# A norm ahead of the block numbers, and routing's second product behind the next transposes

## The chip, the core and the metric

The kernel runs on one core of a Trainium2 chip. The time is the device time of one execution in microseconds. The engines named below are TensorE (PE: matrix products and transposes; PEld is its load of the stationary operand), VectorE (DVE), ScalarE (ACT), GpSimd (POOL) and SyncE (SP, which only issues transfers and reads registers). TensorE writes its results to PSUM, of which the kernel uses 8 banks.

## What is computed

The input x holds 2 sequences of 2048 tokens with 256 channels, in float32. A feed-forward layer, an attention and the same feed-forward layer again are added to it. Cut to what matters:

```python
x = x + 0.5 * ffn(layernorm(x))
x = x + attention(layernorm(x))        # causal, one head of 128
x = x + 0.5 * ffn(layernorm(x))

def ffn(y):
    xln = ln(y, ln1)
    x1 = y + (sigmoid(xln @ Wr) * (xln @ Wv)) @ Wo
    h = ln(x1, ln2)
    conf = sigmoid(h @ [conf_rwkv, conf_trans])          # 3 experts
    bids = conf * shares * sigmoid(h @ w_diff) + h @ W_aff
    w = argmax(bids)                                      # one expert a token
    scale = conf[w] / (conf[w] + 1e-6)
    out = square(relu(h @ K[w])) @ V[w]                   # w = 0, 1
    out = (h @ W1 * sigmoid(xln @ Ws @ W2)) @ W3          # w = 2
    return x1 + out * scale
```

## The kernel before

**Stages.** The feed-forward layer is split. `front` (line 756) does all up to the choice of the expert, in groups of 512 tokens (4 tiles of 128 rows); the two sequences are segments of 4 groups each, so `front` runs over 8 groups, numbered 0 to 7 here. It writes each token's row into a place of its expert in a DRAM table (`move`, an indirect transfer on POOL). `experts` (line 844) then reads blocks of 256 rows that want the same expert, runs the expert and writes the results back by token number. `finish` (line 599) stands at the end of a segment: from the number of tokens of each expert it works out, in some 20 small operations on DVE, `steer`, the numbers of the blocks. SP reads these to address the blocks' rows (`load_rows`, tile `rows_in`). For the first segment that is `finish_whole` (line 626).

**One group in `front`.** While group i is chosen for, group i + 1 is projected and group i + 2 is begun. The steps that this text names:
- `route(0)` (line 464): 8 small products of y_t, the transposed normed rows, with the routing weights, into the sums `ps_rc`. They stay open.
- `rank` for group i - 1: two products, of its winners and of the running counts `upto`.
- `mix`: gate_t times Wo, in two halves `acc`, each a sum over two passes (k = 0, 1). DVE adds them to the rows (line 455).
- `route(1)`: the second product, of gate_t, onto the same `ps_rc`; ACT copies the sum to `by_col` and the token ids to the rows (lines 482, 483).
- `columns` (line 417): 8 transposes of the rows of group i + 1 into two tiles `ps_t`, each copied to `y_t` by ACT.
- `deviation`: moments of the new rows on DVE; `r(0)`: 4 products with Wr and a sigmoid; `start`: moments of group i + 2; `slot`, `move` for group i - 1; `norm2`, `logits`: a transpose of `by_col` (`ps_route`) and small DVE work; `v(0)`: 4 products with Wv, then gate_t on DVE (line 436); `choose`: some 12 small DVE operations ending in `upto`; `r(1)`, `v(1)`.
- At the last group of a segment: `rank`, `slot`, `move` and `finish`.
- `norm1` for group i + 2: six small DVE operations (lines 305 to 318), then its rows are normed on ACT, one tile after another (line 322). Where its group has no row buffer with the input in it, it also has SP copy the input there (line 408, in the second layer).

**Banks.** There are two PSUM pools: `p_mm` with 6 banks (tag "mm") for products and `p_tp` with 2 (tag "tp") for transposes and small sums. A tile waits until one of its pool's banks is free.

**Order.** In the first layer, up to `AHEAD` = 10 steps of `front` beyond the end of the first segment, PE, DVE and ACT keep the order in which the program names the work. From there on a planner orders each engine's work: it plays the program with modelled costs and takes what is ready, what the program names first going first. `front` is a generator; each `yield` ends a step. Beside `experts`, three steps of `front` (`PACE`) go with one of `experts`. In the second layer, `front` for segment 0 is interleaved with the attention of the other sequence. There a row of scores is 128 queries against up to 2048 keys, in up to four tiles `ps_s`; `ps_o` sums the values, and `ps_pt` are the transposes of the probabilities.

Of the kernel before, what the change touches and what calls it, by code (L numbers as in the profile page):

```python
# [8 lines left out]
F32 = mybir.dt.float32  # L9
# [7 lines left out]
P = 128  # L17
# [39 lines left out]
def run(steps):  # L57
    for _ in steps:
        pass
# [20 lines left out]
def kernel(ctx: ExitStack, tc: tile.TileContext, a: dict, out: bass.AP):  # L80
# [6 lines left out]
    GB = T // TG  # L87
# [14 lines left out]
    p_mm = ctx.enter_context(tc.tile_pool(name="p_mm", bufs=6, space=PSUM))  # L102
    p_tp = ctx.enter_context(tc.tile_pool(name="p_tp", bufs=2, space=PSUM))
# [273 lines left out]
    class Group:  # L377
# [86 lines left out]
        def route(self, part):  # L464


            if part == 0:
                self.ps_c = p_tp.tile([P, P], F32, name="ps_rc", tag="tp")
            w, src = ((route_y, self.y_t), (route_g, self.gate_t))[part]
            for k in range(KC):  # L470
                for t in range(TB):
                    nc.tensor.matmul(
                        self.ps_c[t * RC : (t + 1) * RC, :],
                        lhsT=w[:, k, :],
                        rhs=src[:, k, t * P : (t + 1) * P],
                        start=part == 0 and k == 0,
                        stop=part == 1 and k == KC - 1,
                    )
            if part == 0:
                return  # L480
            self.by_col = self.work.tile([P, P], F32, name="by_col")
            nc.scalar.copy(self.by_col, self.ps_c)
            nc.scalar.copy(
                self.rows[:, :, ID], self.seg["ids"][:, self.n * TB : (self.n + 1) * TB]
            )
# [113 lines left out]
    def finish(seg):  # L599

        ps = p_tp.tile([P, E], F32, name="ps_n", tag="tp")
        nc.tensor.matmul(ps, lhsT=ones, rhs=seg["upto"][:, :, ST], start=True, stop=True)
        n_of = sort_pool.tile([P, E], F32, name="n_of")
        nc.vector.tensor_sub(n_of, ps, first[:, :, 0])
        steer = sort_pool.tile([P, STEER], I32, name="steer", bufs=6)

        seg["skip"] = sort_pool.tile([P, STEER], F32, name="skip", bufs=3) if seg["prior"] is not None else None
        if seg["prior"] is None:
            finish_whole(seg, n_of, steer)
        else:  # L610
            for _ in finish_rest(seg, n_of, steer):

                yield from [None] * PACE
        seg["steer"], seg["n_of"] = steer, n_of
        yield
# [140 lines left out]
    def front(work, segs, by_exp=-1, on_move=lambda: None, fill=()):  # L756


        todo = [
            Group(work, seg, n, (b * GB + n <= by_exp, b * GB + n < by_exp)) for b, seg in enumerate(segs) for n in range(GB)  # L760
        ]

        def at(i):
            return todo[i] if 0 <= i < len(todo) else None

        def move(group):
            group.move()
            on_move()

        todo[0].start()  # L770
        run(todo[0].norm1(TB // 2, lately.get("p_tr") if by_exp >= 0 else None))
        yield
        todo[1].start()
        todo[0].columns()
        yield
        for m in range(KC):
            todo[0].r(m)
            yield
            todo[0].v(m)
            yield  # L780
        run(todo[1].norm1(0))
        for i, this in enumerate(todo):
            late, following, further = at(i - 1), at(i + 1), at(i + 2)
            if late and late.n == GB - 1:
                late = None
            this.route(0)
            if late:
                late.rank()
                yield
            this.mix()  # L790
            yield
            this.route(1)
            if following:
                following.columns()
                yield
            this.deviation()
            yield
            if following:
                following.r(0)
                yield  # L800

            if further:
                further.start()
                yield
            if late:
                late.slot()
                with tc.issue_after((further or this).guess):
                    move(late)
                yield
            this.norm2(late.made if late else None)  # L810
            this.logits()
            yield
            if following:
                following.v(0)
                yield
            if following or "gated" not in lately:
                this.choose()
            else:

                for _ in range(PAUSE):  # L820
                    yield
                this.choose(lately["gated"])
            yield
            if following:
                following.r(1)
                yield
                following.v(1)
                yield
            if this.n == GB - 1:

                yield from fill
                if not following:
                    for _ in range(PACE):
                        yield
                this.rank()
                this.slot()
                yield
                move(this)
                yield from finish(this.seg)
            if further:  # L840
                yield from further.norm1(0, following.made)
                yield

    def experts(work, segs, dest, leftovers=False):

# [419 lines left out]
    def until_placed(steps, seg):  # L1265
        while "steer" not in seg:
            next(steps)
            yield
# [5 lines left out]
    def second_half(n, front_pool, segs):  # L1274

        t0, t1 = segs
        with pool(f"attention{n}", "right") as work:
            for g in range(GB):
                x = front_pool.tile([P, TB, C], F32, name=f"x{g}")
                wait_for(nc.sync.dma_start(x, token_tiles(x_mid, GB + g)).ins, s0["results"] + s1["results"])  # L1280
                t1["x"].append(x)
            units = [work.tile([P, TG], F32, name=f"prob{u}") for u in range(5 * GB)]
            xns = [work.tile([P, TB, C], F32, name=f"xn{i}") for i in range(2)]
            xts = [work.tile([P, KC, TG], F32, name=f"x_t{i}") for i in range(2)]
            normed_rows = [r[:, :, YN : YN + C] for r in t0["rows"]]

            def halves(tiles):
                return [t[:, i : i + 2, :] for t in tiles for i in range(0, TB, 2)]


            other = attention(work, t1["x"], units, halves(xns), xns, xts)
            for i, _ in enumerate(attention(work, t0["x"], units, halves(normed_rows[0:2]), xns, xts, normed_rows)):
                if i in NEXT_AT:
                    next(other)
            following = front(front_pool, [t0, t1], by_exp=GB)
            interleave(other, until_placed(following, t0), 9, 8)
            advance(following, AHEAD)
# [10 lines left out]
    with ExitStack() as second:  # L1308
        with pool("experts0", "right") as expert_pool:
            with pool("front0", "left") as front_pool:  # L1310
# [29 lines left out]
                def next_x():  # L1340
                    if waiting:
                        n = waiting.pop(0)
                        fetch(front_pool, s1, n, x_of(1, n), GB + 2)
                        if not waiting:
                            nothing_yet(1)
                            for e in range(E):
                                nc.sync.dma_start(
                                    slot_rows(by_slot[1], e * REGION, NI), blank.unsqueeze(1).to_broadcast([P, NI, RW])
                                )

                following = front(front_pool, [s0, s1], on_move=next_x, fill=folding)
                with tc.manual_schedule(engines={nc.tensor.engine, nc.vector.engine, nc.scalar.engine}):

# [14 lines left out]
                following = until_placed(following, s1)  # L1368
# [76 lines left out]
```

## Time and profile before

The median of 3 runs is 871.15 us (869.32 to 871.39). The profiled execution took 870.89 us by the clock of the runs; its span, from the first to the last instruction, is 869.2 us.

| stage (us from the span's start) | TensorE busy | DVE busy | ACT busy | granted clock |
|---|---|---|---|---|
| first layer, front alone, 28 to 60 (32.0) | 31.62 | 24.55 | 12.53 | 1.00 |
| end of segment 0, 60 to 100 (40.0) | 38.26 | 33.28 | 13.53 | 0.96 |
| front beside experts, 100 to 160 (60.0) | 59.10 | 42.61 | 24.31 | 1.00 |
| experts, 160 to 300 (140.0) | 139.17 | 54.63 | 50.57 | 1.00 |
| attention, 330 to 500 (170.0) | 164.37 | 105.07 | 72.03 | 1.00 |
| attention beside front, 500 to 620 (120.0) | 117.92 | 81.75 | 45.93 | 1.00 |
| front beside experts, 620 to 690 (70.0) | 68.61 | 49.28 | 28.26 | 1.00 |
| experts, 690 to 860 (170.0) | 168.15 | 56.22 | 55.38 | 1.00 |

How to read the lines shown later. A line of the timeline is: start in us, length in us, engine, line of the kernel, operation, what it writes <- what it reads, its size, xcount (how many in a row), and in brackets how long the engine was idle before and what ended that. A matrix product of float32 appears as two instructions, so "x4" for an output of 512 columns are two products. The ends of products are modelled and overlap the next start, so lengths on TensorE are best read from start to start. A line of the page's slices has one digit for a fortieth of the span, the busy share in tenths.

### The profile page before, as it was taken

How to read it: one execution, taken by the hardware profiler on the slowest of the kernel's cores; microseconds unless marked ns; L12 is line 12 of the kernel's file. 1: busy time of each engine (PE TensorE's matmuls, PEld its weight loads, DVE VectorE, ACT ScalarE, POOL GpSimd, SP SyncE). 2: the span in 40 equal slices, each digit the busy share in tenths (PEclk: the TensorE clock that was granted, in tenths of full speed). 3: DMA queues.
4: the chain of work that ended last, by engine and by line, in shares of the span. 5: the costliest groups of instructions: out<-in, count | busy, mean ns of one | idle time of the engine just before them, and what ended most of it. 6: DMA issues, size and time to landing. Idle time of an engine off the chain costs nothing. (4 is left out here: it accounts for less than half of the span.)

```text
span 869.2 us, 12422 instructions
## 1 busy us (share of the span) xinstructions
PE 836.5 (96%) x4136; PEld 612.8 (71%) x4136; DVE 468.8 (54%) x1858; ACT 319.8 (37%) x694; POOL 185.3 (21%) x232
## 2 busy tenths in 40 slices
PE   5999999999999999999999999999999999999995
PEld 4556567888888887555566556556566888888884
DVE  3588866423334645687364777664875523333321
ACT  3243451323443333354363353522362233342311
POOL 3135244311022122000010103033233501112110
PEclk9999999999999999999999999999999999999998
DMA  9924724937269453000000001021373955538641
GB/s 306 373 99 170 266 112 158 365 125 257 91 223 356 170 182 100 0 1 0 1 1 1 1 0 74 25 97 74 130 260 110 370 188 173 191 121 276 216 172 55
DMA packets 69241, 128.09 MB, mean 147 GB/s; under 512 B 4782, under 2 KB 46638, under 8 KB 69168
## 3 DMA queue, kind: packets, MB, share of 16 engines
q1 hardware_dynamic: 58736, 91.93, 31.2%
q0 software_dynamic: 8384, 33.70, 9.7%
q10 hardware_dynamic: 2048, 1.58, 0.6%
q8 instruction: 34, 0.56, 0.3%
q14 instruction: 39, 0.32, 0.1%
HBM read 82.47 MB, written 43.15 MB: 145 GB/s over the span
## 5 line engine op out<-in xcount | busy, mean ns | idle before, releaser
L895 PE MATMUL acc<-w_e,hid 128*128 128x256 f32 x704 | 156.9, 379 | 0.0
L880 PE MATMUL ps_b<-cols,w_k 128*128 128x256 f32 (+1 forms) x768 | 156.5, 362 | 0.0
L880 PEld LDWEIGHTS ps_b<-cols,w_k 128*128 128x128 f32 x768 | 136.4, 190 | 16.6
L895 PEld LDWEIGHTS acc<-w_e,hid 128*128 128x128 f32 x704 | 131.3, 190 | 17.3 <-DVE hid L1023 0.6
L293 POOL TENSOR_TENSOR r<-ve,mhalf 128x4 f32<-128x4 f32 (+1 forms) x40 | 51.3, 1283 | 353.9 <-DVE ve L334 238.2
L1022 ACT ACTIVATE relu<-ps_b 128x512 f32<-128x512 f32 x88 | 52.0, 591 | 165.5 <-PE ps_b L880 163.2
L1023 DVE TENSOR_TENSOR hid<-ps_b,relu 128x512 f32<-128x512 f32 x88 | 60.7, 690 | 77.6 <-ACT relu L1022 76.3
L920 DVE SCALAR_TENSOR_TENSOR res<-acc,rows_in 128x256 f32<-128x256 f32 x68 | 30.2, 479 | 117.4 <-PE acc L895 117.4
L1210 PE MATMUL ps_o<-p_tr,v 128*128 128x512 f32 (+3 forms) x160 | 72.8, 539 | 4.1 <-ACT p_tr L1202 2.3
L572 POOL DMA_INDIRECT by_slot<-rows,slots x64 | 63.0, 985 | 30.3 <-issue 24.8
L928 POOL DMA_INDIRECT out_dram<-res,where x34 | 33.4, 981 | 157.6 <-DVE res L920 133.6
L365 PE MATMUL ps_p<-y_t,w_r 128*128 128x512 f32 x128 | 64.4, 625 | 1.0 <-ACT y_t L420 1.0
L1156 PE MATMUL ps_s<-k_t,q_t 128*128 128x512 f32 (+3 forms) x160 | 64.0, 529 | 0.0
L365 PE MATMUL ps_p<-y_t,w_v 128*128 128x512 f32 x128 | 62.6, 607 | 0.1
L928 POOL DMA_INDIRECT x_mid<-res,where x34 | 33.5, 986 | 133.0 <-DVE res L920 117.0
L446 PE MATMUL acc<-w_o,gate_t 128*128 128x256 f32 x256 | 59.5, 384 | 0.0
L1165 DVE TENSOR_REDUCE top<-ps_s 128x1 f32<-128x512 f32 (+2 forms) x80 | 48.5, 607 | 15.4 <-PE ps_s L1156 14.4
L1173 ACT ACTIVATE prob<-ps_s,shift 128x512 f32<-128x512 f32 (+3 forms) x64 | 38.2, 605 | 43.7 <-DVE shift L1169 43.6
L446 PEld LDWEIGHTS acc<-w_o,gate_t 128*128 128x128 f32 x256 | 47.3, 190 | 7.0 <-issue 0.8
L357 ACT ACTIVATE cols<-ps_bt,lnp 128x256 f32<-128x256 f32 (+1 forms) x96 | 47.3, 553 | 13.2 <-PE ps_bt L864 12.7
L1156 PEld LDWEIGHTS ps_s<-k_t,q_t 128*128 128x128 f32 x160 | 29.2, 190 | 29.3 <-issue 26.3
L283 DVE BATCH_NORM_STATS2 stats<-rows 128x6 f32<-128x256 f32 x128 | 46.3, 412 | 5.0 <-DMA rows<-in_x_dram 5.0
(236 smaller groups left out, 1136.3 us busy)
## 6 DMA issues: line engine op xcount, KB each, us to landing
w_k<-in_K_rwkv_dram SPq DMA_DIRECT2D x24, 1024.0 KB, 6.9
w_e<-in_V_rwkv_dram SPq DMA_DIRECT2D x24, 1024.0 KB, 8.1
rows_in<-by_slot SPq DMA_DIRECT2D x20, 516.0 KB, 6.5
rows_in<-by_slot SPq DMA_DIRECT2D x12, 772.0 KB, 5.5
by_slot<-rows_in SPq DMA_DIRECT2D x6, 772.0 KB, 10.7
rows<-in_x_dram SPq DMA_DIRECT2D x8, 512.0 KB, 5.3
x_mid<-rows_in SPq DMA_DIRECT2D x2, 2048.0 KB, 17.4
rows<-x_mid SPq DMA_DIRECT2D x4, 512.0 KB, 9.5
```

The costliest lines, as they stand in the source:

```text
L293: guess = nc.gpsimd.tensor_tensor(r0[:, 0:n, :], ve[:, 0:n, :], mhalf[:, 0:n, :], ALU.pow)
L365: nc.tensor.matmul(ps, lhsT=w[:, k, m * P : (m + 1) * P], rhs=src_t[:, k, :], start=k == 0, stop=k == KC - 1)
L446: nc.tensor.matmul(acc[:, i, :], lhsT=self.gate_t[:, k, t * P : (t + 1) * P], rhs=w_o[:, k, :], start=k == 0, stop=k == KC - 1,)
L572: nc.gpsimd.indirect_dma_start(out=self.seg["by_slot"], out_offset=bass.IndirectOffsetOnAxis(ap=self.slots[:, t : t + 1], axis=0), in_=sel ...
L880: nc.tensor.matmul(ps[:, j, :], lhsT=w[:, k, (m0 + j) * P : (m0 + j + 1) * P], rhs=cols[:, k, :], start=k == 0, stop=k == KC - 1,)
L895: nc.tensor.matmul(acc[:, i, :], lhsT=src[:, j, i * P : (i + 1) * P], rhs=w[:, j, :], start=j == 0, stop=j == n - 1,)
L928: ins = nc.gpsimd.indirect_dma_start(out=dest, out_offset=bass.IndirectOffsetOnAxis(ap=where[:, i : i + 1], axis=0), in_=res[:, i, :], in_ ...
L1022: nc.scalar.activation(relu, ps, AF.Relu)
L1023: self.made = nc.vector.tensor_mul(self.mid[:, j : j + step, :], ps, relu).ins
L1156: nc.tensor.matmul(ps[:, :w], lhsT=seq["q_t"][:, qi * P : (qi + 1) * P], rhs=seq["k_t"][:, c * TG : c * TG + w], start=True, stop=True,)
L1165: nc.vector.reduce_max(top[:, c : c + 1], ps[:, :w], axis=AX.X)
L1210: nc.tensor.matmul(ps_o[:, i0 * P :], lhsT=seq["v"][:, j, :], rhs=p_tr[:, i0 * P :], start=j == 0, stop=j == blocks - 1,)
```

## The change

Three things are moved.

- `ps_rc` is taken from the pool of 6 banks instead of the pool of 2.
- In each group, `columns` of the next group is named ahead of `route(1)` of this one. So TensorE has the 8 transposes first and then the 16 instructions of the second product, and ACT has the two copies of `y_t` ahead of those of `by_col` and the ids.
- `finish` comes after `norm1` of the group after next instead of before it. That matters at the end of segment 0 alone, since the last group of segment 1 has no group after next. `norm1`'s `yield` now lies before `finish`, so the 10 steps of `AHEAD` begin one step later.

```diff
@@ route
             if part == 0:
-                self.ps_c = p_tp.tile([P, P], F32, name="ps_rc", tag="tp")
+                self.ps_c = p_mm.tile([P, P], F32, name="ps_rc", tag="mm")
@@ front
             this.mix()
             yield
+
+            if following:
+                following.columns()
             this.route(1)
             if following:
-                following.columns()
                 yield
             this.deviation()
             yield
@@ front
                 this.slot()
                 yield
                 move(this)
-                yield from finish(this.seg)
+
             if further:
                 yield from further.norm1(0, following.made)
                 yield
+            if this.n == GB - 1:
+                yield from finish(this.seg)
```

## The prediction

> **What bounds the kernel now.** I read first the page's slices, then TensorE's timeline in the front's stages, then TensorE's waits, then DVE and ACT beside the stage where TensorE waited longest.
>
> ```profile
> PE 836.5 (96%) x4136; PEld 612.8 (71%) x4136; DVE 468.8 (54%) x1858; ACT 319.8 (37%) x694; POOL 185.3 (21%) x232
> ...
> PE   5999999999999999999999999999999999999995
> ```
>
> TensorE is busy from the second slice to the last but one, so a change that leaves its products alone can gain only where it waits. An ordinary front stage of the first layer (group 1) shows one such place:
>
> ```profile
> 45.73 0.64 PE L472 MATMUL ps_rc<-gate_t,route_g 128*32 128x128 f32 x16
> 46.31 1.17 PE L351 MATMUL ps_t<-ident,rows 128*128 128x128 f32 x8
> 47.64 1.98 PE L365 MATMUL ps_p<-y_t,w_r 128*128 128x512 f32 x4 [0.16 <-ACT y_t L420]
> 49.46 0.27 PE L499 MATMUL ps_route<-ident,by_col 128*128 128x128 f32 x1
> ```
>
> From start to start: second routing product 0.58, transposes 1.33, r(0) 1.82. Where nothing holds them, the transposes take 0.95 (597.52 to 598.47) and such a product 1.72 (37.54 to 39.25). 3.73 against 3.25: 0.48 us is lost to the copies of y_t. The stage at the end of segment 0 loses far more:
>
> ```profile
> 85.92 0.15 DVE L604 TENSOR_TENSOR n_of<-ps_n,first 128x3 f32<-128x3 f32 x1
> ...
> 88.88 0.15 DVE L305 TENSOR_TENSOR sq<-r 128x8 f32<-128x8 f32 x1
> ...
> 89.36 0.64 PE L472 MATMUL ps_rc<-gate_t,route_g 128*32 128x128 f32 x16
> ...
> 89.88 1.65 DVE L455 SCALAR_TENSOR_TENSOR rows<-rows,back,acc 128x256 f32<-128x256 f32 x4
> 89.99 2.07 ACT L322 ACTIVATE rows<-rows,shift,rstd 128x256 f32<-128x256 f32 x4 [5.38 <-DVE shift L318]
> ...
> 90.65 0.33 PE L351 MATMUL ps_t<-ident,rows 128*128 128x128 f32 x1 [0.65 <-ACT rows L322]
> ...
> 93.18 3.21 PE L365 MATMUL ps_p<-y_t,w_r 128*128 128x512 f32 x4
> ```
>
> DVE works out the block numbers (L604 on), then the norm's six small operations; ACT, idle for 5.38 us, applies the norm after that, and TensorE waits tile by tile. ps_route follows at 96.22: 6.86 us instead of 3.25, 3.61 lost. The stretches of 3.41 us there:
>
> ```profile
> 88.86:92.27 3.41, 2.28 (x23) 1.10 (x22) 3.31 (x17) 2.28 (x6) 2.04 (x3) 1.00 0.78 307
> 92.27:95.68 3.41, 3.41 (x8) 1.89 (x8) 3.23 (x20) 1.22 (x3) 1.39 (x2) 0.50 0.22 87
> ```
>
> The columns are PE, PEld, DVE, ACT, POOL, then the granted clock: after the stretch in which TensorE was busy for 2.28 us, the clock was 0.50 for 3.41 us, which is 1.7 us of work.
>
> **The change, part by part.**
>
> *Transposes ahead of the second product, its sums in the larger pool.* No instruction is added. The product's 0.58 us now runs while ACT copies y_t (two copies, 1.10 us at 47.00), and the first transposes no longer wait for by_col's copy to free a "tp" bank. The first copy can end some 1.25 us after the transposes start, r(0) starts at 0.95 + 0.58 = 1.53: covered by 0.28; without that cover it costs what is short of it. by_col's copy (0.27) now stands behind both y_t copies on ACT; it ends at about 2.1, ps_route needs it at 3.25, and behind it on ACT stand the copy of the ids and r(0)'s sigmoid, which waits for TensorE until 49.66 anyway. Transposes come 0.58 us sooner after mix, so the norm must be done sooner: in group 1 it was, at 45.06, with mix ending at 45.73. So 0.48 us per group where TensorE has nothing else: groups 0, 1, 3, 5 of layer 1 (group 2: 3.81, so 0.56), groups 4 and 5 of layer 2. Group 6 of either layer, and groups 0 to 3 of layer 2 beside attention, show no gap there: 0.
>
> But DVE takes part of it back:
>
> ```profile
> 54.73 0.77 DVE L535 TENSOR_TENSOR upto<-upto,wins 128x3 f32<-128x3 f32 x4
> ...
> 55.42 0.75 DVE L436 SCALAR_TENSOR_TENSOR gate_t<-ps_p,b_rv,sig 128x512 f32<-128x512 f32 x1
> ...
> 55.64 0.37 PE L542 MATMUL ps_rank<-upto,ones 128*128 128x12 f32 x2
> ```
>
> The rank product needs upto, which DVE finished at 55.50; TensorE got there at 55.64. DVE's chain from mix's sums to here doesn't depend on the transposes, so group 1 gains 0.05 of its 0.48, and group 2 (upto done at 69.23, rank at 69.47) 0.2. Group 0 (DVE idle 0.71 before gate_t) and group 3 (rank at 84.04, upto at 83.05) gain it all. Sum to the end of segment 0: 0.48 + 0.05 + 0.2 + 0.48 = 1.21.
>
> *The norm ahead of the numbers.* Its six operations took 1.02 us in group 1 (41.92 to 42.94). They start at 86.00 - 1.21 = 84.8, ACT runs from 85.9 to 87.95, mix ends at 89.36 - 1.21 = 88.15: the transposes find their rows, by 0.2 us. If that cover is gone, each 0.1 us late costs 0.1. So 3.61 goes, with the half clock. Yet the numbers (85.92 to 88.97, 3.05 us) only change places with the norm: DVE reaches mix's sums no sooner than 89.88 - 1.21 = 88.67. From there to the end of gate_t it took 12.64 us (89.88 to 102.52), of which it was idle for 0.89, 0.96 and 0.35, waiting for TensorE: 10.44 of work. gate_t is ready at 99.1, and mix's second pass needs it 0.43 after mix starts; mix can start at 98.8, against 102.62. TensorE alone would be there at 102.62 - 1.21 - 3.61 = 97.8. So 3.8 us are gained to this point, not 4.8; DVE is late next. Behind the norm in DVE's queue now stand the numbers, and behind these mix's sums; who waits for the sums is the deviation, the logits and gate_t, who waits for the numbers is SP.
>
> Here a rule of the Trainium skill speaks against the change. "TensorE: Matmul & The Clock Gate", Part 1, has the clock fall after at least one *idle* window of about 3.4 us. No such window lies here, so by it the half clock isn't the gap's doing and stays, and 1.7 us less is gained. The row shows the fall right after a window that was two thirds busy; I take the row: no gap, no fall. By the page my sum would be 2.6, by the row 4.3.
>
> The block numbers come 1.02 us later after their product. SP loads them first at 87.6 but issues the first rows_in only at 96.09, waiting for the moved rows: hidden by about 7 us, and it costs the 1.02 if not. The norm's own transfer on SP (L408, in layer 2 only, 0.59 us) was at 608.60, ahead of the numbers' loads, already. POOL's moves stay where they were. AHEAD and PACE now count from one step further on, so the expert blocks enter one front step later.
>
> *After that.* Group 5 would save 0.48, but DVE waits at 104.25 for 0.66 us for rows_in, whose landing moves by 1.21 only while DVE comes some 2.5 sooner. DVE had 2.2 us to spare there (gate_t done at 117.31, mix at 119.55), so I let this wait take the 0.48 and no more; bounds 0 to 1.5 lost. Layer 2: group 4 saves 0.47 (DVE idle 0.43 before gate_t, upto done 1.1 early); its norm ran before the numbers already (L318 at 616.71, L623 at 617.53), so nothing comes of the second move; group 5's saving is taken by the blocks' transposes, which wait 0.61 for DVE and ACT anyway.
>
> *The bank.* ps_rc holds a bank from its first product to by_col's copy: 519.20 to 529 beside attention, again from 561.27 and 589.68. No stage of the trace has it in "mm". Below, gain: TensorE's whole wait from 500 to 620 is 1.9 us. Above, loss: one score row's softmax, about 1.7 us, at each of the three places. I take 0: in these stages TensorE had transposes and value products ready, which need no new "mm" bank. The rule against it is that of "Perfetto Trace Analysis", Matmuls: independent groups should rotate through different banks; for 7 to 10 us five rotate instead of six. By the rule a loss, by the row (96% busy with one "tp" bank left) nothing.
>
> Sum: 3.8 + 0 + 0.47 = 4.3 us. The profiled execution took 870.9 us (span 869.2), so 866.6; the median of the runs shown is 0.26 above it: **866.8 us**. A difference under 0.3%, 2.6 us, is not told from no change.
>
> **Rivals.**
>
> *DVE takes the norm's place entirely.* If the planner sets rows_in's work into DVE's order ahead of mix's sums, the wait at 104.25 grows from 0.66 to some 3 us and the blocks' transposes wait too. For: DVE was busy 13.3 of 16.9 us there. Against: 2.2 us to spare. Gain about 2: 869.2.
>
> *All cover holds.* DVE's side work (L555 to L560, about 0.9) slips behind gate_t, group 5 saves its 0.48 in both layers, and attention's 1.9 us shrink: 6.5 gained, 864.6.
>
> *Slower: five banks beside attention.* In the last quarter a row of scores takes four banks, the value sums one, ps_rc the sixth; mix can't start until an exponential frees one. Price: 1.7 us a place, and as much again if the clock falls: 3.4. One place leaves a gain, two use it up (6.8), three make 10.2, 5.9 more than gained: 877. It decides from the third place on. Against it: the planner may pick other work.
>
> *It doesn't do what it says.* A norm that ACT or the planner holds back anyway leaves 871.
>
> **How the numbers follow.** As worked 0.60 (gain 2.6 to 5.5), all cover 0.12, DVE in its place 0.12, no effect 0.06, slower 0.10. Faster 0.72, same 0.18, slower 0.10. The range 863.8 to 870.0 leaves out the slower case, half of "no effect" and the best few hundredths.
>
> **What would show it.** In the changed profile: no half clock near 92; transposes at about 88 with no wait for ACT L322; r(0) right behind the second product in 1.72; rank or mix waiting for DVE in groups 2, 3 and 5; ps_s or acc not waiting more between 510 and 620. Wrong if the norm still ends after mix, if DVE's chain to gate_t is longer than 10.4, or if a wait of over 2 us stands at ps_bt or mix.

## The result, and the profile after

The changed kernel takes 872.46 us (median of 22 runs), the kernel before 871.15 in the same comparison: a ratio of 1.0025, with a 95% interval of 1.0013 to 1.0037. Instead of the 4.3 us forecast as gain, 1.3 us are lost by the medians and 2.2 by the ratio, which is inside the 0.3% that can't be told from no change, and on the far side of it from the forecast. The profiled execution took 869.98 us (span 868.3), at the quick end of its runs.

The two places that the change aimed at look as it was meant. From TensorE's timeline, group 1's stage after the change:

```profile
43.23 1.04 PE L351 MATMUL ps_t<-ident,rows 128*128 128x128 f32 x8
...
44.19 0.65 PE L472 MATMUL ps_rc<-gate_t,route_g 128*32 128x128 f32 x16
44.77 1.98 PE L365 MATMUL ps_p<-y_t,w_r 128*128 128x512 f32 x4
...
46.59 0.27 PE L499 MATMUL ps_route<-ident,by_col 128*128 128x128 f32 x1
```

From the end of `mix` to `ps_route` it is now 3.36 us (43.23 to 46.59) instead of 3.73. Next the stage at the end of segment 0:

```profile
83.68 0.17 DVE L318 SCALAR_TENSOR_TENSOR shift<-mv,rstd 128x4 f32<-128x4 f32 x1
83.78 0.15 DVE L604 TENSOR_TENSOR n_of<-ps_n,first 128x3 f32<-128x3 f32 x1
83.89 2.08 ACT L322 ACTIVATE rows<-rows,shift,rstd 128x256 f32<-128x256 f32 x4 [2.38 <-DVE shift L318]
...
86.16 1.04 PE L351 MATMUL ps_t<-ident,rows 128*128 128x128 f32 x8
...
87.00 1.65 DVE L455 SCALAR_TENSOR_TENSOR rows<-rows,back,acc 128x256 f32<-128x256 f32 x4
87.12 0.64 PE L472 MATMUL ps_rc<-gate_t,route_g 128*32 128x128 f32 x16
87.70 1.98 PE L365 MATMUL ps_p<-y_t,w_r 128*128 128x512 f32 x4
89.52 0.27 PE L499 MATMUL ps_route<-ident,by_col 128*128 128x128 f32 x1
```

The norm ends (L318) before the numbers begin (L604), the rows are normed at 85.97, the transposes at 86.16 find them, and the granted clock is 1.00 from 60 to 100 us, where it was 0.96 (whether the moved norm did that is taken up below). The loss shows in TensorE's waits of the changed kernel (us in all, times, longest):

```profile
PE ps_rank L541 <- DVE wins L530: 3.8, 2, 1.9
...
PE ps_p L365 <- ACT y_t L420: 1.7, 1, 1.7
```

Neither was there before in this size. The 1.7 us stand in group 5, from the timeline:

```profile
100.00 1.04 PE L351 MATMUL ps_t<-ident,rows 128*128 128x128 f32 x8
100.97 0.64 PE L472 MATMUL ps_rc<-gate_t,route_g 128*32 128x128 f32 x14
101.66 0.42 DVE L997 SCALAR_TENSOR_TENSOR rows_in<-rows_in 128x256 f32<-128x256 f32 x1 [3.75 <-DMA rows_in<-by_slot]
...
102.17 0.60 ACT L998 ACTIVATE rows_in<-rows_in 128x256 f32<-128x256 f32 x1 [2.28 <-DVE rows_in L997]
102.68 1.05 ACT L420 COPY y_t<-ps_t 128x512 f32<-128x512 f32 x2
...
103.29 1.98 PE L365 MATMUL ps_p<-y_t,w_r 128*128 128x512 f32 x4 [1.69 <-ACT y_t L420]
```

DVE stands for 3.75 us at a transfer; behind it in DVE's queue are mix's sums, behind its partner on ACT (L998) the copies of y_t, and for these TensorE waits. The transfer waited for is the third that SP issued (at 94.10, landed at 101.58): the rows are those of the *third* expert block, while the transposes of the first begin at 110.38. The 1.9 us stand in group 7, once in each layer. Here DVE and TensorE in the first layer, after the change:

```profile
142.69 0.16 DVE L530 SCALAR_TENSOR_TENSOR wins<-wins 128x4 f32<-128x4 f32 x1
142.77 0.68 DVE L1016 TENSOR_TENSOR gated<-ps_b,gt_sig 128x512 f32<-128x512 f32 x1
143.00 0.36 PE L541 MATMUL ps_rank<-wins,before 128*128 128x12 f32 x2 [1.89 <-DVE wins L530]
...
143.51 0.70 PE L899 MATMUL acc<-w,gated 128*128 128x256 f32 x2
```

and the same place before:

```profile
145.29 0.69 DVE L1012 TENSOR_TENSOR gated<-ps_b,gt_sig 128x512 f32<-128x512 f32 x1
146.04 1.16 PEld L895 LDWEIGHTS acc<-w,gated 128*128 128x128 f32 x6 [0.65 <-DVE gated L1012]
146.04 1.56 PE L895 MATMUL acc<-w,gated 128*128 128x256 f32 x6 [0.42 <-DVE gated L1012]
146.99 0.16 DVE L530 SCALAR_TENSOR_TENSOR wins<-wins 128x4 f32<-128x4 f32 x1
147.44 0.29 PE L541 MATMUL ps_rank<-wins,before 128*128 128x12 f32 x2
```

Before, DVE made the second block's `gated` and then the choice (L530); TensorE had that block's products `acc` to do while the choice ran. Now the choice is first, TensorE has neither, and waits for both.

How does moving `finish` do that? The last group's choice is named like this (`front`, the kernel's own lines, with two remarks added):

```python
if following or "gated" not in lately:
    this.choose()
else:
    for _ in range(PAUSE):          # PAUSE = 2 * PACE = 6 empty steps
        yield
    this.choose(lately["gated"])    # behind the gated product named last
```

`lately["gated"]` is whatever `experts` has named by then. With `finish` behind `norm1`'s `yield`, `AHEAD` ends one step later and `experts` is one step less far. In the second block `lately["gated"]` used to be that block's product; after the change it is still the first block's, so nothing holds the choice behind the second one any more.

The intervals between like instructions, each from its own profile, in us. ps_route(i) is L499 in group i's stage; w_k is the first product of an expert block with K. Starts from the span's start are left out, since ps_route(0) lies between 32.7 and 36.0 by how soon the first weights land.

| from, to | before | after | PAUSE 7 | PAUSE 7, held | AHEAD 9 |
|---|---|---|---|---|---|
| layer 1: ps_route(0) to (4) | 60.51 | 56.23 | 56.23 | 56.23 | 56.24 |
| (4) to (6): group 5 is here | 31.90 | 34.11 | 34.17 | 31.66 | 31.47 |
| (6) to w_k: group 7 | 20.34 | 22.21 | 20.72 | 20.72 | 20.34 |
| w_k to layer 2's ps_route(4) | 474.65 | 474.02 | 474.36 | 474.22 | 474.37 |
| (4) to (6) | 32.24 | 31.11 | 32.47 | 31.14 | 32.46 |
| (6) to w_k: group 7 | 20.34 | 23.43 | 20.71 | 20.72 | 20.34 |
| w_k to the end | 193.51 | 193.90 | 193.73 | 193.26 | 193.64 |
| sum | 833.49 | 835.01 | 832.39 | 827.95 | 828.86 |

The columns "before" and "after" are the result: 4.28 us gained by ps_route(4), then 2.21 lost in group 5, 1.87 in the last group of layer 1 and 3.09 in that of layer 2; the other three rows add up to 1.37 us of gain. The last three columns are experiments, told below. In layer 1, where the order is the same, an interval repeats to 0.1 us. Layer 2's (4) to (6) does not: a second profile of the changed kernel has 32.38 there instead of 31.11, and one of AHEAD 9 has 31.19 instead of 32.46. In AHEAD 9's first profile the blocks' transposes wait there for 1.32 us for their rows, in the second not at all. So differences of 1.3 us in that row say nothing of the order.

### The profile page after: what moved, and what is told of

It is laid out like the page before. It is cut to its first block, busy times and chain, and to the rows that moved or that the text cites. A ratio compares the mean times of both kernels' runs of the same rounds, so it can differ in the third digit from the quotient of the medians.

```text
span 868.3 us, 12416 instructions
## 1 busy us (share of the span) xinstructions
PE 833.4 (96%) x4136; PEld 614.4 (71%) x4136; DVE 467.3 (54%) x1858; ACT 318.5 (37%) x694; POOL 184.9 (21%) x232
## 5 line engine op out<-in xcount | busy, mean ns | idle before, releaser
L572 POOL DMA_INDIRECT by_slot<-rows,slots x64 | 62.6, 978 | 30.0 <-issue 15.8
L365 PE MATMUL ps_p<-y_t,w_v 128*128 128x512 f32 x128 | 60.4, 593 | 0.0
```

Source lines behind the costliest of these rows:

```text
L365: nc.tensor.matmul(ps, lhsT=w[:, k, m * P : (m + 1) * P], rhs=src_t[:, k, :], start=k == 0, stop=k == KC - 1)
L572: nc.gpsimd.indirect_dma_start(out=self.seg["by_slot"], out_offset=bass.IndirectOffsetOnAxis(ap=self.slots[:, t : t + 1], axis=0), in_=sel ...
```

## The experiments

Theory A: the later entry of the expert blocks costs it all, by two orders that it spoils, group 5's `rows_in` and group 7's choice. Where an expectation names theories B and C, these are rivals by which the later entry by itself costs nothing: B, that the bank costs it; C, that group 5's wait is the whole loss. Ratios are to the kernel before on the same chip, with their 95% intervals.

**Take the later entry back (AHEAD 9), and make it alone (before, with AHEAD 11).**

```diff
 # the changed kernel
-AHEAD = 10
+AHEAD = 9
```

> The changed kernel with AHEAD 9 instead of 10, so that the expert blocks enter at the same step of front as before. Theory A (the loss sits in the last group of each layer: counted one step late, its choose is no longer queued behind gated on DVE, and rank and acc wait for it on TensorE): those two waits of 1.9 us go, with the clock falls they bring; 866.5 to 868.5. Theory B (ps_rc takes a bank from the products): no change, 872 to 873. Theory C (DVE's wait for rows_in in group 5 is the whole loss): 871 to 872.5, with that wait still there.

863.08 us, ratio 0.9927 (0.9908 to 0.9947); in a later comparison with the same kernel (below) 0.9928. One number is worth 8 to 10 us against the changed kernel, more than A had said, and this kernel is faster than both the changed one and the one before; no other here took less time.

```diff
 # the kernel before
-AHEAD = 10
+AHEAD = 11
```

> The kernel before with AHEAD 11 and nothing else changed: only the count of steps is shifted by one. Theory A: the wait of rank for wins appears in the last group of both layers, 1.9 us each and a fall of the clock now and then; 874.5 to 877. Theories B and C: as before, 870.5 to 871.5.

876.55 us, ratio 1.0065 (1.0046 to 1.0083), and its waits hold this line, which the kernel before doesn't have:

```profile
PE ps_rank L541 <- DVE wins L530: 3.8, 2, 1.9
```

The later entry does the harm without any of the rest; B and C fall. But only one of A's two orders is at work here: the last groups take 22.21 and 22.73 us instead of 20.34 twice, while group 5's DVE waits for `rows_in` for no more than 0.45 us. Of the 7.0 us between the two profiles, 4.3 stand in these last groups and 2.0 behind layer 2's w_k, for which no cause is shown.

**The norm's move without and with the later entry.** Both are the kernel before with this edit; the first has AHEAD 9 besides.

```diff
-                yield from finish(this.seg)
             if further:
                 yield from further.norm1(0, following.made)
                 yield
+            if this.n == GB - 1:
+                yield from finish(this.seg)
```

> The kernel before with finish moved behind the norm and AHEAD 9: the norm's move alone, without the swap, without the bank and without the later entry of the blocks. Theory A (the swap gives about 1.5 to 2 us, the norm's move 3.6 to 4.8, each by itself): 865.5 to 867.5, no wait of the transposes for ACT L322 over 0.5 us and no wait of ps_rank. Rival, that the gain of the run with AHEAD 9 (8 us) lies in blocks entering at a better place and not in the norm: 868 or above, with the wait at the segment's end gone all the same.

> The kernel before with finish moved behind the norm and nothing else, so the blocks enter one front step later as in the change. Theory A (the later entry costs 8 to 9 us, the norm's move gains 4 to 5): 873 to 876, with ps_rank in the last group waiting about 1.9 us for DVE in both layers. Rival, that the later entry hurts only together with the swap: 866 to 868, no such wait.

865.90 us, 0.9958 (0.9943 to 0.9973), and 874.73 us, 1.0051 (1.0035 to 1.0068). The move gains 0.42%, 3.7 us; with the step that comes along it loses 0.51%, 4.4 us. Its second kernel shows the wait of 1.9 us twice, and a wait of 3.88 us for `rows_in` in group 5.

**The swap and its bank, without the norm's move.**

```diff
-                self.ps_c = p_tp.tile([P, P], F32, name="ps_rc", tag="tp")
+                self.ps_c = p_mm.tile([P, P], F32, name="ps_rc", tag="mm")
...
+            if following:
+                following.columns()
             this.route(1)
             if following:
-                following.columns()
                 yield
```

> The transposes ahead of the second product and ps_rc in the pool of six, without the moved norm: no shift of steps. By the prediction's own sum 1.2 us to the end of segment 0 and 0.5 to 1.5 in layer 2 are gained, and the stall at the end of segment 0 stays; Theory A: 868.5 to 870. Theory B: the bank costs, 872 to 875. Theory C: 869 to 870.5.

869.36 us, 0.9990 (0.9977 to 1.0002): by itself it can't be told from nothing. Part of what it saves goes into the stall that it leaves at the segment's end; its waits:

```profile
PE ps_t L351 <- ACT rows L322: 3.0, 7, 1.2
```

Before, the same line had 1.1 in all. The transposes come earlier, the norm doesn't. DVE also waits for 2.1 us for `rows_in` in group 5, though the blocks enter at their old step: the later entry is one way to that wait, not the only one. On top of the norm's move the swap gives 0.9927 against 0.9958, 2.7 us; the two intervals, from two comparisons, overlap at their ends, and so how much the swap gives is known roughly.

**Mend the two orders one by one, with the later entry left in.** First the choice: one more empty step, so that `lately["gated"]` is the second block's again.

```diff
-PAUSE = 2 * PACE
+PAUSE = 2 * PACE + 1
```

> The changed kernel with one more empty step ahead of the last group's choose (PAUSE 7 instead of 6), all else as in the change, the rows_in wait in group 5 too. Theory A: choose stands behind gated again, rank doesn't wait; 867 to 868.5. Theory B: 872 to 873. Theory C: 872 to 873.

868.00 us, 0.9975 (0.9964 to 0.9986). No wait at ps_rank; the last groups fall from 22.21 and 23.43 to 20.7. Group 5's wait stays. The order is again that of before, in layer 1 of this kernel's timeline:

```profile
140.77 0.68 DVE L1016 TENSOR_TENSOR gated<-ps_b,gt_sig 128x512 f32<-128x512 f32 x1
...
142.47 0.16 DVE L530 SCALAR_TENSOR_TENSOR wins<-wins 128x4 f32<-128x4 f32 x1
...
142.90 0.29 PE L541 MATMUL ps_rank<-wins,before 128*128 128x12 f32 x2
```

Then group 5 too: the third block's row work is held behind a choice, as the second's was.

```diff
-                yield from block.first(todo[i + 1] if i + 1 < len(todo) else None, i == 0)
+                yield from block.first(todo[i + 1] if i + 1 < len(todo) else None, i <= 1)
```

> The change with PAUSE one step longer (868.0 us as it was run before) and the third block's row work held behind the last choice of experts, as the second block's is already: DVE no longer waits 3.8 us for rows_in ahead of mix's sums in group 5. Theory A (that wait is what is left between 868.0 and the 863.1 with AHEAD 9): 864 to 866, no wait for a DMA at L997 over 1 us between 95 and 106, no wait of ps_p for ACT y_t. Rival, that the rest is lost through the blocks' products standing elsewhere in TensorE's order: 867 to 868.5 with that wait gone.

863.67 us, 0.9941 (0.9923 to 0.9959), just below A's range. Group 5 in this kernel's timeline:

```profile
98.78 0.87 DVE L455 SCALAR_TENSOR_TENSOR rows<-rows,back,acc 128x256 f32<-128x256 f32 x2 [0.99 <-PE acc L446]
...
100.51 1.07 ACT L420 COPY y_t<-ps_t 128x512 f32<-128x512 f32 x2 [0.73 <-PE ps_t L351]
...
101.41 1.98 PE L365 MATMUL ps_p<-y_t,w_r 128*128 128x512 f32 x4
...
124.86 0.42 DVE L997 SCALAR_TENSOR_TENSOR rows_in<-rows_in 128x256 f32<-128x256 f32 x1
```

DVE's sums wait for TensorE, not for a transfer, and the third block's row work comes at 124.86, behind group 6's choice, without any wait. With both orders mended the later entry costs nothing that these runs can tell: 0.9941 against 0.9927.

**Only the hold, and the changed kernel again beside it.** All of these ran on one chip, with AHEAD 9 as well.

> The change with the third block's row work held behind a choice of experts, again beside the changed kernel. Theory A: 0.4 to 0.5% below the changed kernel of this call, ps_rank still waiting for DVE wins twice where the transfers are as in the first profile. Rival, that group 5's time comes back in the last group: within 0.2% of the changed kernel.

> The changed kernel itself, beside the three others of this call on one chip. Where transfers land as in the first profile: 1.0013 to 1.0037 of the kernel before. Where rows_in lands later for every kernel, theory A (the later entry puts the loads of rows_in behind other work, which costs nothing if they are late anyway) has it below 1.000.

> The change with AHEAD 9, again beside the changed kernel. Where transfers land as in the first profile: 0.991 to 0.995 of the kernel before. Where they land later, the wait of the blocks' transposes for rows_in stays, of about 7 us in each layer, in this kernel and in the one before alike, and the ratio is still 0.990 to 0.994.

The changed kernel: 872.17, 1.0038 (1.0019 to 1.0058). AHEAD 9: 863.97, 0.9928 (0.9902 to 0.9954). The hold alone: 873.31, 1.0043 (1.0026 to 1.0061). A missed here, and its rival held: the hold by itself gains nothing, and the wait that A expected at ps_rank is not in its list. Without the longer PAUSE it puts the row work behind *group 7's* choice, and the blocks' transposes wait for it, in the hold's own waits:

```profile
PE ps_bt L868 <- ACT rows_in L998: 6.6, 2, 3.4
```

Group 5's time was taken out (ps_route(4) to (6) is 31.67) and came back in the last groups (25.11 and 25.73 from ps_route(6) to w_k). So the two halves don't add up one by one; what is shown is that with both orders mended the loss is gone.

**The bank.** The kernel with AHEAD 9, with `ps_rc` back in the pool of 2.

> The change with AHEAD 9 (as in the run with AHEAD 9 alone, 863.1 us) and ps_rc back in the smaller pool; nothing else differs, so this is the bank alone. Theory that the bank is worth nothing where TensorE is busy with attention: 862.3 to 864. Rival, that the larger pool pays because by_col's copy comes later with the new order and the first transposes would wait for it: 0.3 to 0.5 us for each of six groups, 865 to 866, and a wait of the transposes or ps_rank for ACT by_col would show. Rival, that five banks beside attention cost something: below 862.

869.31 us, 1.0003 (0.9988 to 1.0017): 6 us worse than with the bank, and above every range expected. In group 1:

```profile
43.74 0.60 PE L351 MATMUL ps_t<-ident,rows 128*128 128x128 f32 x4
44.37 0.58 ACT L420 COPY y_t<-ps_t 128x512 f32<-128x512 f32 x1 [1.23 <-PE ps_t L351]
...
45.01 0.65 PE L351 MATMUL ps_t<-ident,rows 128*128 128x128 f32 x4 [0.68 <-ACT y_t L420]
```

With `ps_rc` open in one of the two banks, the second four transposes wait for the first four to be copied out. But in group 5 this kernel had the planner put the third block's rows early again (DVE waited 4.07 us), so the row work was held here too:

> The change with AHEAD 9, ps_rc back in the smaller pool and the third block's row work held. Theory A: 3 to 4.5 us, 0.35 to 0.5%, above the run with AHEAD 9 of this call, lost group by group to transposes that wait for the copies of y_t. Rival, that the bank by itself is worth nothing: within 1 us of it.

867.26 us, 0.9974 (0.9963 to 0.9984), against 0.9928 for AHEAD 9: the bank is worth 0.46%, 4.0 us (the kernel with AHEAD 9 beside it has no hold, but also no wait in group 5 that a hold could take). Of these, 2.8 us stand from ps_route(0) to (4) of layer 1: 59.04 us against 56.24. Without the bank the swap brings nothing: the norm's move alone takes 57.38 us over the same stages, and has a ratio of 0.9958 (0.9943 to 0.9973).

**Another chip.** Three kernels ran on one where the kernel before took 892.68 us.

> The change with one edit: the third block's row work held behind a choice of experts. Theory A (the wait for rows_in ahead of mix's sums costs about 4 us, the last group's choice ahead of gated about 4, each by itself): 867 to 869, no wait of ps_p for ACT y_t in group 5, ps_rank still waiting 1.9 us for DVE twice. Rival, that group 5's time comes back as a longer wait in the last group: 871 to 872.5.

> The change with AHEAD 9 and the third block's row work held as well. In the run with AHEAD 9 alone that work stood where nothing waited for it, so theory A expects no difference: 862.3 to 864. Rival, that later row work leaves DVE freer ahead of gate_t: 861 to 862.

> The change with AHEAD 9 and ps_rc in the smaller pool (869.3 us as it was run before), and now the third block's row work held behind a choice of experts, so that DVE's wait of 4.1 us for rows_in ahead of mix's sums is out of it. What is left against 863 is the bank by itself. Theory A (0.5 to 0.9 us in each of the six groups where TensorE has nothing else, by transposes waiting for the copies of y_t): 866 to 867.5. Rival, that nearly all of the 6 us was the wait for rows_in: 863 to 864.5. Rival, that the hold changes nothing there: 869.

0.9912 (0.9895 to 0.9929), 0.9912 (0.9888 to 0.9937) and 0.9984 (0.9971 to 0.9998), at 885.12, 884.28 and 890.60 us. TensorE waited far longer for the blocks' rows there; the waits of AHEAD 9 with the hold:

```profile
PE ps_bt L868 <- ACT rows_in L998: 15.5, 2, 7.7
```

AHEAD 9 had 1.5 us in this line on the chip of its first run. Why the rows came late isn't shown: the loads of rows between 120 and 175 us landed 15.0 us after their issue in this kernel, but 9.1 with the hold alone on the same chip, and 3.5 to 15.8 us with AHEAD 9 on its own. Waits of that size may cover others, so these runs are not used for the two orders. The last two kernels differ by the bank alone, and it pays here as well: 0.9912 against 0.9984. The hold alone, 0.4% slower than the kernel before in the comparison above, is 0.9% faster here. The changed kernel itself was not run on that chip, so what the later entry costs there stays open; the gains and losses above are those of the other chips.

## Why the prediction was wrong

The step that failed is its sentence on `AHEAD`: "AHEAD and PACE now count from one step further on, so the expert blocks enter one front step later." It was stated, and no price was worked out for it. The sum took 0; AHEAD 9 against the changed kernel says 0.98% in one comparison and 1.10% in the other, 8.5 and 9.6 us. What the step does, and the prediction nowhere asked, is to change which instructions the planner holds back and which not: in the last groups DVE makes the choice ahead of `gated`, and TensorE waits 1.89 us in each layer; in group 5 DVE waits 3.75 us for rows ahead of `mix`'s sums. The profiles show 1.49 and 2.72 us in the last groups and 2.51 in group 5 (table, "after" to "PAUSE 7" to "held"), 6.7 together, of which 1.2 are a half clock.

The rest is most likely the clock, which differs from one execution to the next; no profile of a slower one shows it. The changed kernel's 22 runs spread from 869.05 to 876.5 us: the eight with a mean granted clock of 0.995 or more took at most 872.47, the three with 0.987 or 0.988 at least 875.24. Over all 22 the mean is 0.9926, over the six of AHEAD 9 it is 0.9963. That is 0.0037 of 870 us, an estimate of 3.2 us; with the 5.5 us of order that are no half clock it makes 8.7. (Every profile also has a half clock in its last 5 to 9 us, where TensorE has no work left and it costs nothing. In the profiles of these two kernels it makes 2.6 to 3.2 us of lost clock, so it isn't the difference.)

- *The swap.* To ps_route(4), with the segment's end: forecast 1.21 + 3.61, less group 0's 0.48, which lies ahead of ps_route(0), so 4.34; measured 4.28. Layer 2's group 4: forecast 0.47, measured 0.46 (13.75 to 13.29). A small miss: r(0) took 1.82 to ps_route, not 1.72, so 0.37 and not 0.48 were saved in a stage by itself.
- *The norm ahead of the numbers, and the clock.* ps_route(3) to (4) fell from 19.16 to 15.57, 3.59 of the 3.61, with the clock at 1.00 throughout. By the Trainium skill's rule ("TensorE: Matmul & The Clock Gate", Part 1: at least one idle window) the half clock would have stayed in this stage; it did not. Yet the gap doesn't decide it alone: the swap by itself kept a longer wait in this place (1.7 us instead of 1.1), and the clock stayed at 1.00 (last section). So the 1.7 us were gained in this profile, but that the moved norm brought them is not shown. The price by the page was also wrong: 1.7 us off the sum left out that DVE was to be late by 1.0 anyway (TensorE at 97.8 + 1.7 = 99.5 against 98.8), so 0.7 less, not 1.7.
- *DVE is late next.* Right in kind: mix's sums to the end of the second gate_t took 9.88 us (87.00 to 96.88), forecast 10.44. Mix of group 5 ended 4.30 us earlier, counted from group 0's first routing product, forecast 3.8 (99.1 less 0.43 is 98.7 and not 98.8, so by its own figures 3.9).
- *Group 5.* "bounds 0 to 1.5 lost" was too narrow: 2.2 lost against before, 2.6 against AHEAD 9. The rival "DVE takes the norm's place entirely" described this wait (3 us forecast, 3.75 measured, a gain of only 2 left), and was given 0.12 because DVE had 2.2 us to spare. But its cause was the place in the order, not DVE's load: with AHEAD 9 and the same norm the wait is not there.
- *The bank beside attention.* Taken as 0; the stage ps_route(3) to (4) of layer 2 grew from 17.84 to 18.67, where `ps_o` waits 1.09 us for ACT's `p_tr` instead of 0.35, one place and 0.8 us. It is the bank: the profiles on these chips with `ps_rc` in the larger pool have 18.54 to 18.76 us there, those with it in the smaller one 17.56 to 18.14. The other stages beside attention didn't grow. Its real worth, 4 us in all and 2.8 of them in layer 1's first groups, wasn't in the prediction, which named the bank that the transposes no longer wait for but gave it no price of its own.
- *The sum without the failed step.* Forecast 4.3; AHEAD 9 gives 4.63 in its profile from ps_route(0) on, some 5.1 with group 0, and 6.4 us (4.6 to 8.0) by the ratio.

## What to carry to other kernels

When an edit moves a `yield`, list every place whose order is taken from "what was named last", and work out for each which instruction that will now be; a step of no cost of its own was worth 6 us in the kernel before and 8 to 10 in the changed one. The hold was worth nothing alone and 3 to 4 us with the longer PAUSE, so test a part with the others in place as well as alone. And work put early can be dear: row work that nobody needed yet, ahead of sums, stopped DVE for 3.75 us and ACT for 2.28.

## What was unexpected of the hardware

The clock fell in layer 2 after the wait in group 7, and not after the same wait in layer 1. The stretches of the changed kernel (PE, PEld, DVE, ACT, POOL, granted clock, DMA share, GB/s):

```profile
139.60:143.01 3.41, 1.52 (x10) 1.14 (x9) 2.17 (x14) 1.14 (x3) 2.64 (x3) 1.00 0.93 275
143.01:146.42 3.41, 3.26 (x17) 2.77 (x18) 3.06 (x24) 0.00 (x0) 2.78 (x3) 1.00 0.97 316
...
668.48:671.89 3.41, 1.42 (x8) 1.13 (x9) 2.75 (x20) 1.14 (x3) 2.50 (x4) 1.00 1.05 344
671.89:675.30 3.41, 3.41 (x11) 2.78 (x10) 2.92 (x24) 0.00 (x0) 2.67 (x3) 0.50 1.03 360
```

And one of the swap alone, at the end of segment 0:

```profile
88.50:91.91 3.41, 1.70 (x8) 0.73 (x8) 3.31 (x15) 2.07 (x4) 1.92 (x2) 1.00 0.78 310
```

In the changed kernel TensorE was busy for 1.52 and 1.42 of 3.41 us; only the second was followed by a half clock, for 1.2 us more lost (22.21 against 23.43 in the table). In its second profile layer 2 has the same wait, 22.21 and no fall. In the swap alone no fall followed a stretch of 1.70 us, while in the kernel before one followed a stretch of 2.28 in the same stage. So a wait of about 2 us may bring a half clock or not in the same program, and the longer wait isn't the one that brings it; by which rule these runs don't show.
